# Sorted edge groups in pairs, selected by quarters, with 16-bit destinations and one 16-bit bias pass

## The chip, the core and the metric

The program runs on one core of one Trainium2 chip. A core has a matrix engine (PE, with its weight loads shown as PEld), a vector engine (DVE), a scalar engine (ACT), a third compute engine (POOL, which here issues the indirect gathers) and a sync engine (SP, which here issues DMAs). Each engine works through its own list of instructions in order and waits on semaphores. The metric is the device time of one execution in microseconds (us); lower is better.

## The reference

A graph layer with 6,250 nodes, 100,000 edges sorted by destination, 128 features and 4 edge attributes, in 32-bit floats:

```python
msg_in = concatenate([x[src], x[dst], edge_attr], axis=1)
h = silu(msg_in @ mW1 + mb1)
aggregated = segment_sum(h @ mW2 + mb2, dst, num_segments=6250)
u = silu(concatenate([x, aggregated], axis=1) @ uW1 + ub1)
out = _layernorm(x + layer_norm(x + u @ uW2 + ub2, ln_g, ln_b))
```

Here `layer_norm` normalises over the features, scales by `ln_g` and adds `ln_b`, and `_layernorm` is the same without scale and shift.

## The kernel before

The first product is split: table A is `x @ mW1[:128]` and table B is `x @ mW1[128:256] + mb1`, each with one row for each node. Edges are cut into 98 groups of 1,024 (`GE`), each of 8 tiles of 128. Because destinations are sorted, the destinations of a group lie in a window of 80 rows (`W`) of table B, and its sums go into a window of 80 columns of an accumulator.

There are two ways to get a group's rows of table A.

- A *listed* group (78 of them) gathers: eight indirect DMAs on POOL (`fetch`, line 243) bring 128 rows each. PE adds the destination part and the attributes (`before_rows`, `pre<-mv,st`: a one-hot matrix `st` of the destinations, made by DVE at line 603 from the row `near`, times 80 rows of table B). DVE adds the two (line 655), ACT applies silu (line 657), and `sums` multiplies the result by the one-hot matrix `oh` into `pt`, which `add` puts into the accumulator.
- A *sorted* group (20 of them, every fourth from 15 on: `Q0, QD, QN = 15, 4, 20`) has its edges sorted by source at the start of the run, so that the edges of each tile of 128 source nodes lie in a narrow window of positions (`window`, line 119). PE then selects rows without a gather: for every tile `b` of 128 nodes that can occur, it multiplies the tile of table A by a one-hot matrix `O` of the keys, over the columns of the window, into the bank `po`. Table A is held as three 16-bit parts, so each window takes three products (`select`, line 1080). The position range is cut into two halves of 512, and a window that crosses the cut is worked in two pieces.

The one-hot matrices `O` of a sorted group are made by `picks` (two of four by DVE at line 1052, two by ACT at lines 1056 and 1057). Its attributes enter through `attribute_part` (a 512-wide 32-bit product of `at_s` and `Oc`, and a DVE step at line 1068 that writes into `st_s`), the destination part through `begin_half`; silu is at line 1099, and `turned_hidden` transposes the result back (line 1107) and copies it (line 1108).

The order is written out by hand. The loop at line 1212 has one stage for each listed group. In a stage the loads for later groups are issued on SP (`sorted_ahead`, then `load`), then come the matrices of the group two ahead, `before_rows` and `hidden` of the next one, the pieces of a sorted group (`sorted_before`), the sums of this group, `sorted_behind`, and steps for a batch of 512 nodes (`node_stage`). A sorted group `k` is spread over the six stages before its own place: loads six stages ahead, matrices five, first attribute part four, both quarters of the first half three, one quarter of the second half two, the last quarter one stage ahead, sums at its place. So its pattern has a period of three stages, in which four groups are done. Gathers are paced: `paced` (line 1277) ties every second one to a product on PE some 3.5 groups earlier.

Once for each batch of nodes (line 735) `node_y` opens a bank with the bias row `ub2`: a 32-bit product of a row of ones with a row that holds `ub2` four times.

Of the kernel before, what the change touches and what calls it, by code (L numbers as in the profile page):

```python
# [10 lines left out]
F32 = mybir.dt.float32  # L11
# [10 lines left out]
P = 128  # L22
# [5 lines left out]
def kernel(  # L28
# [57 lines left out]
    Q0, QD, QN = 15, 4, 20  # L86
    by_sort = {Q0 + QD * q: q for q in range(QN)}
# [6 lines left out]
    SORTED = Q0 - 7  # L94
    S0 = 96
    HB = GE // 2
    SLACK = 400.0
# [13 lines left out]
    def made_for(g):  # L111
        stage = stage_of(g) - 5 if g in by_sort else turn_of(g) - LEAD
        return max(k for k in range(NB) if k < 2 or x_stage(k) + 2 < stage)
# [5 lines left out]
    def window(b, half):  # L119
# [4 lines left out]
        lo = max(floor(edge(b * P, -1)), half * HB)  # L124
        hi = min(ceil(edge(min(b * P + P - 1, N - 1), 1)) + 1, half * HB + HB)
        return lo, hi
# [106 lines left out]
    sd = dram.tile([4, QN * GE], F16, name="sd")  # L233
    ea_d = dram.tile([ED, NG * GE], F32, name="ea_d")
# [97 lines left out]
    def lists_1():  # L332
# [4 lines left out]
        nc.vector.tensor_scalar(rel_n, dst_l, base_c, None, op0=OP.subtract)  # L337
        parts.update(base_c=base_c, rel_n=rel_n, rel_t=rel_t)
# [101 lines left out]
    def destinations(g):  # L440
        near[g] = work.tile([P, GE], I32, name="near")[:W]
        n = min(GE, E - g * GE)
        if n < GE:
            nc.vector.memset(near[g][:, n:], N)
# [85 lines left out]
    ub2_row = consts.tile([1, BN, H], F32, name="ub2_row")  # L530
    late = {}

    def weights():
# [4 lines left out]
        nc.sync.dma_start(mb2_col, mb2.rearrange("(f o) -> f o", o=1))  # L538
        nc.sync.dma_start(
            ub2_row, ub2.rearrange("(o i f) -> o i f", o=1, i=1).to_broadcast([1, BN, H])  # L540
# [5 lines left out]
    def merged():  # L546
# [9 lines left out]
        nc.scalar.copy(bc_row, pb[0:1, :H])  # L556

# [6 lines left out]
    for k in range(NST + 1):  # L564
        ohbuf.append(kept.tile([P, G, WS if k < NST else W], F32, name=f"oh{k}"))
# [33 lines left out]
    def matrices(g):  # L599
        if g >= NG:  # L600
# [5 lines left out]
            base_p[:W, g : g + 1],  # L606
# [128 lines left out]
    def node_y(k):  # L735
# [3 lines left out]
        matmul(py[:, :n], ones[0:1, :], ub2_row[:, :n], start=True, stop=False)  # L739
# [81 lines left out]
    def turned_lists():  # L821
        pt = selected()
        for f, of in enumerate((src_i, rel)):
            picked = first.tile([P, QN, G], F32, name="picked")
            nc.vector.tensor_copy(picked, of[:, Q0 : Q0 + QN * QD : QD, :])
# [135 lines left out]
    def prepare():  # L961
        pool = edges.enter_context(tc.tile_pool(name="sel", bufs=1, side="right"))
        t = {
            "O": lambda: pool.tile([P, G // 2, HB], BF16, name="O", bufs=3),
            "sc": lambda: pool.tile([P, 2, GE], F16, name="sc", bufs=2),
            "ar": lambda: pool.tile([P, GE], F16, name="ar"),
            "h": lambda: pool.tile([P, G, H], F32, name="h_s"),
            "hT": lambda: pool.tile([P, HB], F32, name="hT", bufs=2),
        }
        t["Oc"] = pool.tile([P, GE], F32, name="Oc")  # L970
        t["st"] = pool.tile([P, GE], F32, name="st_s")
        t["mv"] = [pool.tile([P, H], F32, name=f"mv_s{k}") for k in range(2)]
        t["at"] = pool.tile([P, P], F32, name="at_s")
        nc.vector.memset(t["st"][S0 - 32 : S0], 0.0)
        for m in t["mv"]:
            nc.vector.memset(m[S0 - 32 : S0], 0.0)
        nc.vector.memset(t["at"][:, :S0], 0.0)
# [34 lines left out]
    def load_sorted(g):  # L1012
        t, q = sel[0], by_sort[g]
        cols = slice(q * GE, (q + 1) * GE)
        now["sc", g] = t["sc"]()
        nc.sync.dma_start(
            now["sc", g], sd[0:2, cols].rearrange("(o f) e -> o f e", o=1).to_broadcast([P, 2, GE])
        )
        now["ar"] = t["ar"]()
        nc.sync.dma_start(now["ar"][:W], sd[3:4, cols].to_broadcast([W, GE]))  # L1020
        nc.sync.dma_start(now["ar"][S0:], sd[2:3, cols].to_broadcast([P - S0, GE]))
        nc.sync.dma_start(
            t["at"][:, S0:],
            edge_attr[g * GE : (g + 1) * GE].rearrange("(c a) d -> c (a d)", a=G),
        )

    def load_rows(g):
        t, q = sel[0], by_sort[g]
        need_bases(g)
        nc.sync.dma_start(t["mv"][q % 2][:W], tab_b[bass.ds(bases[g], W), :])  # L1030

    def sorted_matrices(g):
        t = sel[0]
        nc.vector.tensor_scalar(
            t["st"][:W],
            now["ar"][:W],
            p_col[:W],
            0.0,
            op0=OP.is_equal,
            op1=OP.add,  # L1040
            accum_out=deg_col(g),
        )
        nc.vector.tensor_scalar(t["Oc"], now["sc", g][:, 1], p_col, None, op0=OP.is_equal)

    def picks(g, c):
        half, r0 = c // 2, c % 2 * (G // 2)
        O = sel[0]["O"]()
        key = now["sc", g][:, 0, half * HB : (half + 1) * HB]
        for j in range(G // 2):
            r = r0 + j  # L1050
            if j < 2:
                nc.vector.tensor_scalar(  # L1052
                    O[:, j], key, p_rows[:, r : r + 1], None, op0=OP.is_equal
                )
            else:
                nc.scalar.activation(O[:, j], key, AF.Square, bias=p_less[:, r : r + 1])  # L1056
        nc.scalar.activation(O[:, 2:], O[:, 2:], AF.Relu, bias=ones[:, 0:1], scale=-1.0)  # L1057
        now[c] = O
# [494 lines left out]
```

## Time and profile before

| what | value |
|---|---|
| median of 3 runs | 1014.65 us (1009.31 to 1018.19) |
| time of the profiled execution | 1012.41 us |
| its span, first to last instruction | 1010.6 us |
| mean granted PE clock | 0.896 |
| PE busy / weight loads busy | 812.3 us / 694.0 us, 7154 instructions each |
| DVE / ACT / POOL busy | 581.8 / 456.9 / 612.4 us |
| DMA moved | 108.69 MB |

The page's busy times of PE are those of instructions whose ends are modelled, and neighbours overlap; the distance between the starts of two products says more. In a group's row the mean duration of one follows the busy time, then the idle time of the engine just before such instructions and what ended most of it; "issue" there means that the engine waited for nothing that the profile shows.

### The profile page before, as it was taken

How to read it: one execution, taken by the hardware profiler on the slowest of the kernel's cores; microseconds unless marked ns; L12 is line 12 of the kernel's file. 1: busy time of each engine (PE TensorE's matmuls, PEld its weight loads, DVE VectorE, ACT ScalarE, POOL GpSimd, SP SyncE). 2: the span in 40 equal slices, each digit the busy share in tenths (PEclk: the TensorE clock that was granted, in tenths of full speed). 3: DMA queues.
4: the chain of work that ended last, by engine and by line, in shares of the span. 5: the costliest groups of instructions: out<-in, count | busy, mean ns of one | idle time of the engine just before them, and what ended most of it. 6: DMA issues, size and time to landing. Idle time of an engine off the chain costs nothing.

```text
span 1010.6 us, 19484 instructions
## 1 busy us (share of the span) xinstructions
PE 812.3 (80%) x7154; PEld 694.0 (69%) x7154; DVE 581.8 (58%) x1464; ACT 456.9 (45%) x685; POOL 612.4 (61%) x633
## 2 busy tenths in 40 slices
PE   5557546888988878978978978878989888978884
PEld 4547536676777677767767768667777687767673
DVE  3465687964564664744755654754764664654464
ACT  1122113563545545545554554564554564454343
POOL 6656655866666665666665666666666666565650
PEclk8769777888999999988998999999989989899977
DMA  9554323542443443533533533542533633423321
GB/s 219 136 146 113 100 72 78 139 128 76 120 116 95 121 117 94 133 99 89 137 100 82 148 97 89 139 114 78 162 94 86 149 93 93 122 60 86 91 61 30
DMA packets 87568, 108.69 MB, mean 108 GB/s; under 512 B 22044, under 2 KB 63504, under 8 KB 87466
## 3 DMA queue, kind: packets, MB, share of 16 engines
q1 hardware_dynamic: 54194, 60.01, 21.6%
q0 software_dynamic: 19904, 40.80, 16.8%
q10 hardware_dynamic: 13368, 6.56, 2.4%
q8 instruction: 58, 0.95, 0.4%
q14 instruction: 44, 0.36, 0.1%
HBM read 95.88 MB, written 11.43 MB: 106 GB/s over the span
## 4 chain that ended last, share of the span: by engine, by line
PE 64%; issue 13%; DVE 11%; ACT 4%; another core or an unknown queue 3%; DMA 2%; SPq 1%; POOL 1%; DVEq 1%; ACTq 0%; POOLq 0%
PE po L152 22%; PE pt L152 16%; PE pre L152 12%; PE pn L152 10%; PE pn L155 2%; DVE ga L655 2%; PE pre L155 1%; DVE y L760 1%; ACT O L1056 1%; DVE bn L716 1%; DVE z L785 1%; ACT O L1057 1%; DVE var L717 1%; DMA near<-in_dst_dram 1%
## 5 line engine op out<-in xcount | busy, mean ns | idle before, releaser
L243 POOL DMA_INDIRECT ga<-tab_a,src_i x582 | 572.4, 983 | 349.9 <-issue 155.9
L152 PE MATMUL po<-O,A_low 128*128 128x144 bf16 (+25 forms) x1120 | 209.7, 227 | 11.2 <-issue 11.2
L152 PE MATMUL po<-O,A 128*128 128x147 bf16 (+37 forms) x1720 | 177.5, 230 | 39.1 <-issue 22.8
L152 PE MATMUL pre<-mv,st 128*128 128x128 f32 x1244 | 179.0, 293 | 25.8 <-DVE st L603 8.2
L152 PEld LDWEIGHTS pre<-mv,st 128*128 128x128 f32 x1244 | 164.2, 206 | 39.5 <-issue 17.9
L152 PEld LDWEIGHTS pt<-oh,h 128*128 128x128 f32 x1244 | 164.7, 208 | 34.4 <-issue 32.5
L152 PE MATMUL pt<-oh,h 128*128 128x104 f32 x1244 | 173.0, 293 | 18.5 <-issue 14.2
L152 PEld LDWEIGHTS <-A 128*128 128x128 bf16 x1720 | 144.2, 106 | 57.4 <-issue 56.1
L703 DVE TENSOR_TENSOR acc<-acc,pt 128x80 f32 x98 | 23.0, 234 | 275.2 <-PE pre L152 120.4
L657 ACT ACTIVATE h<-ga 128x512 f32<-128x512 f32 x146 | 88.8, 627 | 190.4 <-DVE ga L655 108.9
L152 PEld LDWEIGHTS <-A_low 128*128 128x128 bf16 x1120 | 115.4, 104 | 16.7 <-issue 16.6
L655 DVE TENSOR_TENSOR ga<-ga,pre 128x512 f32<-128x512 f32 x146 | 94.3, 676 | 32.0 <-PE pt L152 9.0
L603 DVE TENSOR_SCALAR_CACHE_REDUCE st<-near,base_p 80x1024 f32<-80x1024 int32 x78 | 98.4, 1261 | 14.5 <-issue 9.2
L1056 ACT ACTIVATE O<-sc,p_less 128x512 bf16<-128x512 f16 x160 | 105.5, 706 | 0.0
L1057 ACT ACTIVATE O<-O,ones 128x1024 bf16<-128x1024 bf16 x80 | 91.8, 1148 | 2.6
L1099 ACT ACTIVATE hT<-po 128x512 f32<-128x512 f32 x40 | 23.5, 587 | 108.3 <-PE po L152 39.9
L613 DVE TENSOR_TENSOR oh<-w_row,rel 128x640 f32<-128x640 f32 x78 | 63.6, 816 | 0.6
L152 PE MATMUL po<-O,A_high 128*128 128x51 bf16 (+12 forms) x520 | 49.4, 217 | 16.6 <-issue 16.4
L152 PEld LDWEIGHTS <-A_high 128*128 128x128 bf16 x520 | 38.0, 99 | 28.9 <-issue 28.9
L243 POOL DMA_INDIRECT ga<-in_x_dram,src_i x40 | 38.3, 957 | 23.0 <-issue 10.4
L152 PE MATMUL pn<-Oc,at_s 128*128 128x512 f32 x80 | 47.9, 683 | 4.1 <-issue 4.1
L1052 DVE TENSOR_SCALAR O<-sc,p_rows 128x512 bf16<-128x512 f16 x160 | 49.8, 362 | 0.0
(221 smaller groups left out, 921.0 us busy)
## 6 DMA issues: line engine op xcount, KB each, us to landing
near<-in_dst_dram SPq DMA_DIRECT2D x77, 320.0 KB
sc<-sd SPq DMA_DIRECT2D x20, 512.0 KB
ga<-tab_a,src_i POOLq DMA_INDIRECT x582
ar<-sd SPq DMA_DIRECT2D x20, 160.0 KB
mv<-tab_b SPq DMA_DIRECT2D x78, 40.0 KB
tab_a<-A SPq DMA_DIRECT2D x11, 256.0 KB
tab_b<-o SPq DMA_DIRECT2D x11, 256.0 KB
out_dram<-o ACTq DMA_DIRECT2D x11, 256.0 KB
```

The source lines that it names most:

```text
L152: counted(nc.tensor.matmul(to, *operands, **flags), to, share)
L155: counted(nc.tensor.transpose(to, *operands), to)
L243: ins = nc.gpsimd.indirect_dma_start(out=rows[g][:, i, :], out_offset=None, in_=x if g < RAW else tab_a[:, :], in_offset=bass.IndirectOffs ...
L603: nc.vector.tensor_scalar(stbuf[turn_of(g) % NST][:W], near.pop(g), base_p[:W, g : g + 1], 0.0, op0=OP.is_equal, op1=OP.add, accum_out=deg ...
L613: nc.vector.tensor_tensor(oh[g][:, :n, :W], w_row[:, None, :].to_broadcast([P, n, W]), rel[:, g, :n, None].to_broadcast([P, n, W]), op=OP. ...
L655: nc.vector.tensor_add(s[:, i], s[:, i], of)
L657: nc.scalar.activation(h[:, i], of, AF.Silu)
L703: nc.vector.tensor_add(to, to, pt[:, :W])
L1052: nc.vector.tensor_scalar(O[:, j], key, p_rows[:, r : r + 1], None, op0=OP.is_equal)
L1056: nc.scalar.activation(O[:, j], key, AF.Square, bias=p_less[:, r : r + 1])
L1057: nc.scalar.activation(O[:, 2:], O[:, 2:], AF.Relu, bias=ones[:, 0:1], scale=-1.0)
L1099: nc.scalar.activation(now["hT", half], now.pop("po"), AF.Silu)
```

## The change

Sorted groups are now neighbours, two at a time: 17 and 18, 25 and 26, up to 89 and 90. They are still 20. A pair is worked together, by four quarters of 256 positions of each of the two groups. One product covers the same window in both groups: its columns are two runs, one in each. A pair is spread over stages 8 to 0 before its place, and the pattern has a period of six stages, in which eight groups are done. Quarter `u` is loaded at `at_stage[u] + 3`, its matrices are made at `+ 2`, its one-hot matrices and attribute part at `+ 1`, and it is selected 5, 4, 2 and 1 stages ahead.

Three smaller edits go with it. The destinations relative to a group's first one are written once to DRAM as 16-bit floats, and `near` is loaded from there (it was loaded as 32-bit integers from `dst`), so line 603 compares with `p_col` and not with `base_p`. The bias row `ub2` is held as three 16-bit parts on three partitions, and the opening product of `node_y` is one 16-bit pass. Buffers: `O` has four (three before), `st_s` and `at_s` two each, `ar` two, `h_s` is for two groups, `oh` has one more.

```diff
-    Q0, QD, QN = 15, 4, 20
-    by_sort = {Q0 + QD * q: q for q in range(QN)}
+    Q0, QD, QN = 17, 8, 20
+    firsts = [Q0 + QD * q for q in range(QN // 2)]
+    by_sort = {k + u: 2 * q + u for q, k in enumerate(firsts) for u in range(2)}
...
+    QB = GE // GR
+    at_stage = (5, 4, 2, 1)
...
+        rel_h = first.tile([P, GE], F16, name="rel_h")
+        nc.scalar.copy(rel_h[:NG], rel_n)
+        nc.sync.dma_start(near_d, rel_h[:NG])
...
-        nc.sync.dma_start(
-            near[g][:, :n],
-            dst[g * GE : g * GE + n].rearrange("(o e) -> o e", o=1).to_broadcast([W, n]),
-        )
+        near[g] = work.tile([P, GE], F16, name="near")[:W]
+        nc.sync.dma_start(near[g], near_d[g : g + 1].to_broadcast([W, GE]))
...
+        rows = late.pop("rows")
+        part = first.tile([96, H], BF16, name="ub2_part")
+        nc.scalar.copy(ub2_rows[0:1], rows[0:1])
+        nc.scalar.copy(part, rows)
+        nc.vector.tensor_sub(rows, rows, part)
+        nc.scalar.copy(ub2_rows[32:33], rows[32:33])
+        nc.scalar.copy(part, rows)
+        nc.vector.tensor_sub(ub2_rows[64:65], rows[64:65], part[64:65])
...
-        matmul(py[:, :n], ones[0:1, :], ub2_row[:, :n], start=True, stop=False)
+        matmul(
+            py[:, :n], ones_16, ub2_rows[:, None, :].to_broadcast([P, n, H]),
+            start=True, stop=False, share=1 / 4,
+        )
...
+    def load_part(k, u):
...
+        for f in range(2):
+            nc.sync.dma_start(
+                sc[:, f], of[f].rearrange("(o g) c -> o g c", o=1).to_broadcast([P, 2, QB])
+            )
...
+    def sorted_matrices(k, u):
         t = sel[0]
+        for v in range(2):
+            nc.vector.tensor_scalar(
+                t["st"][u % 2][:W, v * QB : (v + 1) * QB],
+                now["ar", u][:W, v],
+                p_col[:W],
+                0.0,
+                op0=OP.is_equal,
+                op1=OP.add,
+                accum_out=t["deg"][:, v, u : u + 1],
+            )
...
+        if u == GR - 1:
+            for v in range(2):
+                nc.vector.tensor_reduce(deg_col(k + v), t["deg"][:, v], AX.X, OP.add)
...
+    def select(u):
         t = sel[0]
+        po = now["po"] = selected()
+        for v in range(2):
+            cols = slice(v * QB, (v + 1) * QB)
+            matmul(po[:, cols], t["mv"][v], t["st"][u % 2][:, cols], start=v == 0, stop=False)
+        to = po.rearrange("p (g c) -> p g c", g=2)
         todo = []
...
+        for part_r in range(2):
+            O = now.pop(("O", u, part_r)).rearrange("p r (g c) -> p r g c", g=2)
+            r0 = part_r * (G // 2)
+            for b in range(NT):
+                if r0 <= b % G < r0 + G // 2:
+                    lo, hi = window(b, u)
+                    if lo < hi:
+                        cols = slice(lo - u * QB, hi - u * QB)
+                        for a in parts_of(b):
+                            todo.append((to[:, :, cols], a, O[:, b % G - r0, :, cols]))
+        for n, (to, a, of) in enumerate(todo):
+            matmul(to, a, of, start=False, stop=n == len(todo) - 1, share=1 / 3)
...
     def sorted_before(j):
...
+        for u, d in enumerate(at_stage):
+            for _ in pair_at(j, d + 1):
+                picks(u)
+        for k in pair_at(j, 0):
+            for v in range(2):
+                add(k + v, sums(k + v))
+        for u, d in enumerate(at_stage):
+            for k in pair_at(j, d - 1):
+                if u < GR - 1:
+                    turned_hidden(k, u)
+        for u, d in enumerate(at_stage):
+            for _ in pair_at(j, d):
+                select(u)
+                sorted_hidden(u)
+        for u, d in enumerate(at_stage):
+            for _ in pair_at(j, d + 1):
+                attribute_part(u)
+        for k in pair_at(j, 1):
+            for v in range(2):
+                sorted_oh(k + v)
```

More of the change, by code (lines that the diff above doesn't have):

```diff
@@ L1045, in picks @@
[L1045 to L1058, printed above, removed]
+            ar[S0:], of[2].rearrange("(o g) c -> o g c", o=1).to_broadcast([P - S0, 2, QB])
+        )
@@ new lines, in picks @@
+    def picks(u):
+        key = now.pop(("sc", u))[:, 0].rearrange("p g c -> p (g c)")
+        for part_r in range(2):
+            O = sel[0]["O"]()
+            for j in range(G // 2):
+                r = part_r * (G // 2) + j
+                if j < 2:
+                    nc.vector.tensor_scalar(
+                        O[:, j], key, p_rows[:, r : r + 1], None, op0=OP.is_equal
+                    )
+                else:
+                    nc.scalar.activation(O[:, j], key, AF.Square, bias=p_less[:, r : r + 1])
+            nc.scalar.activation(O[:, 2:], O[:, 2:], AF.Relu, bias=ones[:, 0:1], scale=-1.0)
+            now["O", u, part_r] = O
```

209 lines of the change are left out of this document (86 added, 123 removed).

## The prediction, made before the changed kernel was run

> **What bounds the kernel now.** I read the page first, then the engines' busy time between the 13th and the 73rd listed group, then single selections in the timeline, then the waits of PE and POOL.
>
> ```profile
> PE 812.3 (80%) x7154; PEld 694.0 (69%) x7154; DVE 581.8 (58%) x1464; ACT 456.9 (45%) x685; POOL 612.4 (61%) x633
> ...
> PE 64%; issue 13%; DVE 11%; ACT 4%; another core or an unknown queue 3%; DMA 2%; SPq 1%; POOL 1%; DVEq 1%; ACTq 0%; POOLq 0%
> ...
> L243 POOL DMA_INDIRECT ga<-tab_a,src_i x582 | 572.4, 983 | 349.9 <-issue 155.9
> L152 PE MATMUL po<-O,A_low 128*128 128x144 bf16 (+25 forms) x1120 | 209.7, 227 | 11.2 <-issue 11.2
> L152 PE MATMUL po<-O,A 128*128 128x147 bf16 (+37 forms) x1720 | 177.5, 230 | 39.1 <-issue 22.8
> ...
> L152 PE MATMUL po<-O,A_high 128*128 128x51 bf16 (+12 forms) x520 | 49.4, 217 | 16.6 <-issue 16.4
> ```
>
> The chain that ended last is PE for 64%, and 13% of the span (131 us) is "issue", time in which the waiting engine waited for nothing visible. The selections are 1120 + 1720 + 520 = 3360 products, 168 for each sorted group.
>
> ```profile
> core 0: us, PE busy (x) PEld busy (x) DVE busy (x) ACT busy (x) POOL busy (x), PEclk, DMA share, GB/s
> ...
> 213.00:960.30 747.30, 646.96 (x6124) 548.66 (x6122) 418.25 (x1002) 377.52 (x565) 465.98 (x479) 0.94 0.41 106
> ```
>
> From the sums of the 13th listed group at 213.0 to those of the 73rd at 960.3 there are 60 stages, ten times eight groups: 74.7 us for eight groups, my unit below. Only PE looks full, but what is it full of? The starts of products in two selections tell:
>
> ```profile
> 416.38 0.20 PE L152 MATMUL po<-O,A 128*128 128x19 bf16 x2
> ...
> 416.46 0.20 PE L152 MATMUL po<-O,A 128*128 128x40 bf16 x2
> ...
> 417.03 0.30 PE L152 MATMUL po<-O,A 128*128 128x156 bf16 x2
> ...
> 417.23 0.30 PE L152 MATMUL po<-O,A 128*128 128x155 bf16 x2
> ```
> ```profile
> 429.27 0.21 PE L152 MATMUL po<-O,A_high 128*128 128x51 bf16 x2
> ...
> 431.25 0.23 PE L152 MATMUL po<-O,A 128*128 128x78 bf16 x2
> ...
> 431.87 0.23 PE L152 MATMUL po<-O,A 128*128 128x57 bf16 x2 [0.35 <-issue]
> ...
> 432.62 0.21 PE L152 MATMUL po<-O,A 128*128 128x36 bf16 x2 [0.49 <-issue]
> ...
> 433.33 0.18 PE L152 MATMUL po<-O,A_low 128*128 128x36 bf16 x1 [0.50 <-issue]
> ...
> 434.78 0.22 PE L152 MATMUL po<-O,A_high 128*128 128x110 bf16 x1 [1.14 <-issue]
> ```
>
> Three products of 156 columns take 0.20 us, 67 ns each (0.43 ns a column); three of 19 columns take 0.08 us, 27 ns each. So PE pays by the column down to about 27 ns. The second selection runs like that from 429.27 for 13 windows (39 products, 78 instructions with their loads) and then stops: at 431.87, 432.62, 433.33 and 434.78 it sits idle, after only three to five products each time. No semaphore is named. I read this as instructions arriving late: a run of narrow products uses them up at about 78 in 2.6 us, 30 per us, and then gets some 8 to 10 per 0.7 us, 13 per us. Over the 747.3 us PE took 6124 products and as many loads, 16.4 per us: the whole stretch goes at close to the rate of the starved part.
>
> ```profile
> PE po L152 <- issue: 46.9, 81, 2.3
> PE po L152 <- ACT O L1057: 16.0, 8, 2.3
> PE pt L152 <- issue: 11.3, 20, 1.1
> PE pre L152 <- DVE st L603: 5.6, 5, 3.7
> PE pn L155 <- DVE st_s L1068: 5.2, 4, 2.4
> PE pre L152 <- issue: 4.7, 10, 0.9
> ```
>
> In the same stretch such gaps end 111 waits of PE, 62.9 us beyond the modelled ends. A product's row lasts about 0.2 us where the next could start after 0.05, so each gap hides some 0.15 us more: 62.9 + 111 x 0.15 = 80 us, 8 for eight groups. Semaphores account for 16.0 + 5.6 + 5.2 = 26.8 us, 2.7 for eight groups.
>
> **Eight groups on PE, from rows.**
>
> ```profile
> 478.62 0.91 PE pn L152 x8
> ...
> 488.90 2.99 PE pn L152 x6
> 491.88 1.78 PE pre L152 x16
> ...
> 495.97 0.94 PE pn L152 x2
> 496.91 1.76 PE pt L152 x16
> 498.67 3.02 PE pn L152 x12
> 501.69 0.44 PE pn L155 x4
> ```
>
> Six listed groups: 6 x (1.78 + 1.76) = 21.2. Two sorted ones: sums 80 and not 104 columns wide, 2 x 1.35 = 2.7; four 512-wide attribute products 4 x 0.94 = 3.8 and four destination products of that shape, 3.8; four transposes 1.8; selections: the window formula gives 19,587 columns a group, 2 x 19,587 x 0.43 ns = 16.8, with the 27 ns floor of narrow pieces 17.5. One batch of nodes: 2.99 + 0.91 + (3.02 - 0.94) + 0.44 (four transposes of x) + 0.2 (the transposed counts) = 6.6. Sum 57.4 of 74.7. The other 17.3: the granted clock of 0.94 means half speed in 12% of the time, 4.5 us; semaphores about 3; the gaps 8; 2 not assigned.
>
> **The change, part by part.**
>
> *Selection.* By the window formula the columns stay exactly the same (39,174 a pair). The pieces go from 56 a group (112 a pair) to 70 a pair, so products from 336 to 210 a pair and from 3360 to 2100 in all: 117 columns each before, 187 after, 0.08 us for two instructions, 25 per us. By columns alone that is worth only the floors of narrow pieces, 0.4 us a pair. By instructions, eight groups go from 622 products (counted in the code; 612 a unit recorded) to 622 - 126 + 16 (destination and attribute products are cut in two) - 1 = 511, 82%. A selection is now at most 57 products, 114 instructions in 4.8 us, where two quarters used to run together, 84 products. Take 13 to 16.4 per us as the supply; then 78 - 2.6 x 13 = 44 to 78 - 2.6 x 16.4 = 35 were in store, and 4.8 us have 44 + 4.8 x 13 = 106 to 35 + 4.8 x 16.4 = 114 of the 114: just enough, or one gap. I take 2 us of gaps for eight groups in place of 8, and 1 of the 2 unassigned. Bounds: all 8 stay, or none. A product over two runs of columns does not occur before; its bounds are no cost and one floor more, 210 x 27 ns = 5.7 us a pair. I take no cost, since pieces of 19 to 156 columns show no price beyond columns and floor.
>
> The Trainium skill, TensorE: Matmul & The Clock Gate, section Back-to-back issue gap, gives columns/2.4 + 2.5 ns between matmuls at full clock; the dense rows agree (156 columns: 67.5 ns). By that rule alone the pairing is worth 126 x 2.5 ns, an estimate of 0.3 us a pair: it speaks against this change.
>
> *Row ub2.* Two 512-wide passes of 0.94 / 2 become one 16-bit pass, 512 x 0.43 ns = 0.22: 0.7 us a batch, one batch a unit.
>
> *DVE.*
>
> ```profile
> L1034 DVE TENSOR_SCALAR_CACHE_REDUCE st_s<-ar,p_rows x20: 1264/1268/1271, 191.1 to 905.4; 80x1024 f32<-80x1024 f16 x20
> L1043 DVE TENSOR_SCALAR Oc<-sc,p_rows x20: 740/745/892, 192.3 to 906.6; 128x1024 f32<-128x1024 f16 x20
> ```
>
> A pair had 2 x (1.27 + 0.08 + 0.75) = 4.2 us of these; it gets eight 256-wide ones (0.32 by size, at most 0.6; I take 0.45, plus 0.08), four 512-wide ones (0.37 to 0.75; 0.5) and two small reductions (0.2): 6.6 us, 2.4 more, at the end of four of six stages. DVE goes from 41.8 to 44.2 us a unit, two thirds of 66: hidden behind PE, except where PE waits for the next `st`; 0.5 us. The first row reads 16 bits and takes what line 603 takes for 32, so the new `near` saves nothing on DVE.
>
> *ACT.* `picks` and silu keep their number and size. They come as two `O` in each of four stages: 2 x (2 x 0.71 + 1.15) = 5.1 us beside silu and copies of 2.4, 7.5 of an 11 us stage, selected one stage later as before. The late steps of a node batch (tables, output) fall four stages before a pair's place, where no `picks` stands. I leave its wait, 1.6 us a unit, as it is.
>
> *SP and DMA.* A pair's DMAs on SP go from 10 to 20, about 0.35 us each to issue: 3.5 us a unit on an engine that mostly waits. They stand ahead of `load` in each stage and wait for `ar` and `sc` of two quarters before, free by the end of the stage before; `near`, `mv` and `st` behind them are needed a stage later. Cover: that stage, 11 us; without it the landing, 2 to 3 us, would show in DVE's `st` and so in `pre`. `near` moves half the bytes. I take 0 (bounds -1 and +3 us a unit).
>
> *Start.* A copy to 16 bits (about 1 us on ACT), one 200 KB store that the first `near` waits for, and seven small steps for `ub2` (about 2.5 us): once, beside the tables; 0, at most +6. The ends of the run keep their stages.
>
> **Sum.** 57.4 - 0.4 - 0.7 = 56.3; clock 4; semaphores 3 + 0.5; gaps 2; unassigned 1: 66.8, and I take 66 because gaps also bring on the low clock. 74.7 - 66 = 8.7, times ten: 87 us. The profiled execution took 1012.41 us (0.2% under the median of 1014.65): 1012.4 - 87 = 925 us.
>
> **Gathers beside it.**
>
> ```profile
> 402.52 0.94 POOL L243 DMA_INDIRECT ga<-tab_a,src_i  x1 [0.30 <-issue]
> ...
> POOL ga L243 <- remote: 42.4, 31, 1.7
> ```
>
> A gather costs at least 0.94 + 0.30 us; by the mean 0.98 + 0.30, 48 for eight groups are 61.4 us, 65.7 with the unknown waits of 42.4 / 10. That is late next: under 66 the gathers set the pace, so little more than forecast is to be had.
>
> **Rivals.**
>
> *The gaps stay.* If they do not come from the number of instructions (another engine's traffic, a place in the program), pairing saves 0.4 + 0.7 us a unit: 1012 - 11 = 1001, from 990 to 1010. For it: 84-product runs sometimes pass without a gap. Against it: gaps sit after some 80 instructions of a dense run, with no semaphore. The Trainium skill, Runtime: NRT & Kernel Launch, section Instruction fetch mechanics, holds that fetching is hidden, since dispatch (some 20 cycles an instruction) is slower than the refill; by that rule this rival is right, and the rows at 431.87 to 433.33 do not look like it.
>
> *Gathers bound.* If they stay at 65.7 and meet PE's waits badly, some 69 a unit: 1012 - 57 = 955.
>
> *Slower: `O` comes late.* Two `O` take 5.1 us of ACT in a stage where one or two stood. If each of a pair's four selections waits more than 8.7 / 4 = 2.2 us for ACT, the gain is gone; at 3.5 us each it is 14 - 8.7 = 5.3 a unit, 1012 + 53 = 1065. For it: the wait is there now (16.0 us, up to 2.3). Against it: ACT is busy for 377.52 of 747.30 us.
>
> **Chances.** Forecast 0.66 (own range 895 to 960), gathers bound 0.09, gaps stay 0.15, slower 0.10. About 1% is what a measurement of this kernel tells from no change. Faster by over 1% (under 1004.5): 0.66 + 0.09 + a third of 0.15 = 0.80; within 1% 0.09; slower 0.11. The low end, 890, is gathers without a wait (61.4 a unit: 1012 - 133 = 879) nearly reached; the high end, 1000, takes in most of "the gaps stay".
>
> **What would show it.** Right: 2100 selection products, their idle time by "issue" down from 50.4 us (11.2 + 22.8 + 16.4) to under 20; granted clock above 0.90; POOL's share of the span at 66% or more. Wrong: "issue" unchanged beside 2100 products; `po` waiting for ACT over 40 us; a product over two runs taking visibly more than its columns.

## The result: slower, and where the time went

| | before | changed |
|---|---|---|
| median of 4 runs each | 1016.42 us (1009.31 to 1018.29) | 1077.88 us (1074.53 to 1082.12) |
| profiled execution, its span | 1012.41, 1010.6 us | 1078.77, 1077.0 us |
| mean granted PE clock | 0.896 | 0.859 |

The ratio is 1.062 (95% interval 1.058 to 1.067): some 62 us slower, where 87 us faster was forecast. The page of the changed kernel (busy times, the chain of waits) and its groups by line show it; line numbers moved, so the matmul helper is now line 155, transposes are line 158, the add into the accumulator is line 716.

```profile
PE 817.7 (76%) x6041; PEld 720.4 (67%) x6041; DVE 594.5 (55%) x1629; ACT 458.4 (43%) x690; POOL 611.0 (57%) x633
...
PE 54%; DVE 19%; issue 12%; another core or an unknown queue 6%; POOL 3%; ACT 2%; DMA 2%; DVEq 1%; ACTq 0%; POOLq 0%; SPq 0%
```
```profile
L155 PE MATMUL po<-O,A_low 128*128 128x314 bf16 (+54 forms) x700 | 156.0, 246 | 7.1 <-issue 6.9
L155 PE MATMUL po<-O,A 128*128 128x216 bf16 (+37 forms) x1060 | 143.8, 246 | 12.9 <-issue 12.8
...
L155 PE MATMUL po<-O,A_high 128*128 128x102 bf16 (+16 forms) x340 | 46.3, 246 | 4.3 <-issue 4.3
```

The selections did what the change says: 700 + 1060 + 340 = 2,100 products, with 24.0 us of idle time by "issue" where the three rows of before sum to 50.4. But the chain of waits runs 19% through DVE (11% before) and 54% through PE (64%). The list of PE's waits (us in total, times, longest) names what is new:

```profile
PE pn L158 <- DVE st_s L1109: 45.5, 10, 6.0
PE pt L155 <- DVE acc L716: 30.1, 10, 5.1
PE po L155 <- issue: 24.0, 43, 1.1
...
PE pn L155 <- DVE Oc L1078: 22.7, 8, 3.3
```

Three waits of PE for DVE, 45.5 + 30.1 + 22.7 = 98.3 us, each about once for each of the ten pairs. In the same list of before, `st_s` stands with 5.2 us, the wait for `acc` with 2.4 and Oc not at all. And over ten units, from the sums of the 13th listed group to those of the 73rd, the unit grew from 74.7 to 80.9 us, with the granted clock down from 0.94 to 0.89:

```profile
core 0: us, PE busy (x) PEld busy (x) DVE busy (x) ACT busy (x) POOL busy (x), PEclk, DMA share, GB/s
212.40:1021.70 809.30, 653.57 (x5035) 574.81 (x5033) 431.04 (x1154) 377.84 (x565) 461.51 (x480) 0.89 0.34 87
```

The first theory was therefore: the selections became shorter, and the order of the pair's stages made round trips between PE and DVE (PE waits until DVE has read its bank, and only then goes on) that nothing covers. Stages are named here by their distance d to the pair's place. The pair selects at d = 5, 4, 2 and 1, and not at 3 and 0. At the end of d = 4 and in d = 3 DVE has the second normalisation of a node batch, in d = 0 PE has two sums of the pair through the one buffer of `pt`. The experiments take these apart.

### The profile page after: what moved, and what is told of

The parts are those of the page before. It is cut to its first block, busy times and chain, and to the rows that moved or that the text cites. A ratio compares the mean times of both kernels' runs of the same rounds, so it can differ in the third digit from the quotient of the medians.

```text
span 1077.0 us, 17602 instructions
## 1 busy us (share of the span) xinstructions
PE 817.7 (76%) x6041; PEld 720.4 (67%) x6041; DVE 594.5 (55%) x1629; ACT 458.4 (43%) x690; POOL 611.0 (57%) x633
## 4 chain that ended last, share of the span: by engine, by line
PE 54%; DVE 19%; issue 12%; another core or an unknown queue 6%; POOL 3%; ACT 2%; DMA 2%; DVEq 1%; ACTq 0%; POOLq 0%; SPq 0%
PE po L155 16%; PE pt L155 14%; PE pre L155 12%; PE pn L155 8%; POOL ga L247 3%; PE pn L158 3%; DVE ga L668 2%; DVE O L1092 2%; DMA ga<-tab_a,src_i 2%; DVE st L616 2%; DVE oh L626 1%; DVE bn L729 1%; DVE z L801 1%; DVE var L730 1%
## 5 line engine op out<-in xcount | busy, mean ns | idle before, releaser
L155 PE MATMUL po<-O,A_low 128*128 128x314 bf16 (+54 forms) x700 | 156.0, 246 | 7.1 <-issue 6.9
L155 PE MATMUL po<-O,A 128*128 128x216 bf16 (+37 forms) x1060 | 143.8, 246 | 12.9 <-issue 12.8
L155 PEld LDWEIGHTS <-A 128*128 128x128 bf16 x1060 | 88.6, 97 | 32.1 <-issue 18.1
L616 DVE TENSOR_SCALAR_CACHE_REDUCE st<-near,p_rows 80x1024 f32<-80x1024 f16 x78 | 98.4, 1262 | 11.0 <-issue 9.8
L1109 DVE SCALAR_TENSOR_TENSOR st_s<-ar,part,pn 32x512 f32<-32x512 f16 x40 | 30.2, 756 | 117.1 <-PE pn L155 83.7
L155 PEld LDWEIGHTS <-A_low 128*128 128x128 bf16 x700 | 67.6, 98 | 18.5 <-issue 11.8
L155 PE MATMUL pt<-oh,h_s 128*128 128x80 f32 x320 | 51.3, 323 | 35.2 <-DVE acc L716 29.8
L155 PEld LDWEIGHTS pt<-oh,h_s 128*128 128x128 f32 x320 | 47.9, 235 | 37.8 <-DVE acc L716 31.1
L155 PE MATMUL pn<-Oc,at_s 128*128 128x256 f32 x160 | 52.3, 457 | 25.6 <-DVE Oc L1078 22.7
L155 PEld LDWEIGHTS pn<-Oc,at_s 128*128 128x128 f32 x160 | 31.8, 221 | 30.6 <-remote 23.3
```

Of the source, the lines that this page charges most:

```text
L155: counted(nc.tensor.matmul(to, *operands, **flags), to, share)
L616: nc.vector.tensor_scalar(stbuf[turn_of(g) % NST][:W], near.pop(g), p_col[:W], 0.0, op0=OP.is_equal, op1=OP.add, accum_out=deg_col(g),)
L1109: nc.vector.scalar_tensor_tensor(t["st"][u % 2][S0:], now.pop(("ar", u))[S0:].rearrange("p g c -> p (g c)"), part[S0:], px[S0:], op0=OP.is ...
```

## Experiments on the parts

All ratios are to the kernel before on the same chip; differences of ratios are turned into us with 1016. The first four ask which part costs.

**e1: the same pairs, each product cut in two again**

```diff
-                            todo.append((to[:, :, cols], a, O[:, b % G - r0, :, cols]))
+                            for v in range(2):
+                                todo.append((to[:, v, cols], a, O[:, b % G - r0, v, cols], share))
```

> The changed kernel with each selection product over two groups cut again into one product for each group: 4,200 products in place of 2,100, the same columns in the same order, everything else as it is. Theory (the loss comes from round trips between PE and DVE that the grouping into pairs creates, and the number of products matters only inside the selections): the idle time of the selections by 'issue' comes back from 24 to 50 us or more and the time rises by 20 to 70 us, because PE is the bound in the stages that select, while the waits of PE for DVE (x transposes 45.5 us, second sums 30.1, Oc 22.7) stay or shrink by the slack that PE loses. Rival (the number of instructions is worth nothing and fewer products saved nothing): within 10 us of the changed kernel. Rival (the two-run product itself is slow and is the loss): the split kernel is faster than the changed one by 30 us or more.

Ratio 1.102 (1.096 to 1.107), so 40 us above the changed kernel; the selections' idle time by "issue" went to 72.0 us, and of the three waits for DVE that for Oc is down to 0.4 us; that the longer selections cover it is the likely reason and was not tried alone. The pairing of products saves something here, and all else that came with the pairs costs at most about 100 us (1.102 against 1; e1 has 840 products more than the kernel before, and their price is in it).

**e2: the small edits alone, on the kernel before**

```diff
-        near[g] = work.tile([P, GE], I32, name="near")[:W]
+        near[g] = work.tile([P, GE], F16, name="near")[:W]
+        nc.sync.dma_start(near[g], near_d[g : g + 1].to_broadcast([W, GE]))
...
-        matmul(py[:, :n], ones[0:1, :], ub2_row[:, :n], start=True, stop=False)
+        matmul(
+            py[:, :n], ones_16, ub2_rows[:, None, :].to_broadcast([P, n, H]),
+            start=True, stop=False, share=1 / 4,
+        )
```

> The kernel before with the two small edits alone: destinations in 16 bits from DRAM, and the row ub2 by one 16-bit pass; no pairs. Theory (the loss is all in the pairing): 0 to 12 us faster than before, about 1008. Rival (the 16-bit destinations bring a longer start or later one-hot matrices, and with them a part of the loss): slower than before by 10 us or more.

Ratio 0.999 (0.996 to 1.003). Together they cost nothing and bring nothing that can be seen; the loss is in the pairs.

**e3: both sums of a pair, then both adds**

```diff
-            for v in range(2):
-                add(k + v, sums(k + v))
+            both = ps1.tile([P, 4 * P], F32, name="pt")
+            half = [both[:, 2 * P * v : 2 * P * v + 2 * P] for v in range(2)]
+            for v in range(2):
+                sums(k + v, half[v])
+            for v in range(2):
+                add(k + v, half[v])
```

> The changed kernel with the sums of both groups of a pair in two halves of one bank, both sums first and then both adds, in place of sum, add, sum, add through one buffer. Theory (each DVE round trip is a wait that nothing covers): the wait of the second sums for the first add (30.1 us, ten times 3) is gone and the time falls by 15 to 30 us, to about 1053. Rival (PE only runs up against something else, such as the gathers or DVE's total): the 30 us show up in other waits and the time stays within 8 us.

Ratio 1.035 (1.030 to 1.040): 28 us less than the changed kernel, as the theory said. The wait itself fell from 30.1 to 13.8 us and did not vanish: what is left stands before the next group's sums, which take the same bank after both adds.

**e4: the second normalisation one stage later**

```diff
-            if j == u + 2:
+            if j == u + 3:
                 r = inverse(0, 2 * BN, k)
                 node_z(k, r)
```

> The changed kernel with the second normalisation of a node batch (DVE's inverse and node_z, and ACT's output steps) one stage later, so that it ends in front of a stage that selects, not in front of the stage without a selection. Theory: the x transposes' wait for DVE (45.5 us in ten) falls under 15 and the time falls by 20 to 40 us. Rival (the wait comes from the selection's own DVE work, picks and attribute part, and not from the node batch): the wait stays over 30 us and the time within 8 us. Third possibility: the wait only moves to the stage after, same time and another line in the list of waits.

Ratio 1.037 (1.032 to 1.041), 26 us less. The waits show that the theory holds for the larger part only:

```profile
PE pn L155 <- remote: 25.0, 8, 3.3
PE pn L158 <- issue: 24.8, 11, 5.4
...
PE pn L158 <- DVE st_s L1109: 10.7, 6, 3.7
```

The transposes' wait for DVE fell from 45.5 to 10.7 us. The row with "remote" is the wait for Oc under another name: its eight products begin 0.15 us after the end of Oc's step, as the eight of the changed kernel do. The 24.8 us in front of transposes are new, and the list names no cause; in the trace eight of these eleven waits, 23.0 us, are transposes of a selection's result that begin 0.05 us after ACT has ended its silu (line 1137). So a part of the wait went over to ACT.

**e5 and e6: a third bank for `pn`, and its control**

For a third bank the row of column numbers leaves the bank that it has to itself; e5 does that alone.

```diff
-    w_row = ps1.tile([P, W], F32, name="w_row")
+    w_row = kept.tile([P, W], F32, name="w_row")
...
-        return ps1.tile([P, BN, P], F32, name="pn", bufs=2)
+        return ps1.tile([P, BN, P], F32, name="pn", bufs=3)
```

> Control for the next run: the changed kernel with the row of column numbers (`w_row`, 80 numbers that DVE compares with) in SBUF in place of a PSUM bank of its own; nothing else. Theory and rivals agree: within 8 us of the changed kernel (ratio to before 1.055 to 1.070), the waits of PE as they are.

> As the control, with the bank that came free given to `pn`, which so has three buffers in place of two. Theory (the x transposes stand still because the bank they want is held until DVE has done the step of attribute_part): their wait of 45.5 us falls under 10 and the time falls by 20 to 45 us against the control. Rival (PE would only wait a little later for the same DVE work): the wait is gone from this row and comes back on other rows, with the time within 8 us of the control.

Control 1.072 (1.068 to 1.076), with the third bank 1.036 (1.028 to 1.043): 37 us between them. The control is itself some 10 us above the changed kernel, a little more than expected, so e6 lies 27 us under the changed kernel. No wait of the x transposes for `st_s` is left in the list of e6 (42.6 us in e5): what they waited for was the bank.

**e7: all pairs one group later**

```diff
-    Q0, QD, QN = 17, 8, 20
+    Q0, QD, QN = 18, 8, 20
```

> The changed kernel with the first pair at group 18 in place of 17, all pairs one group later, so that the node batches (every eighth group) fall one stage earlier within a pair's six stages; nothing else. The node batch's DVE work then runs into a stage that selects. Theory: the x transposes' wait for DVE falls under 15 us and the time falls by 15 to 45 us. Rival (any order of these stages has the same waits, the pairs alone are the cause): within 8 us of the changed kernel.

Ratio 1.016 (1.012 to 1.020): one number, 47 us less, a little over the range. No row for x transposes that wait for `st_s` is left in the list, and Oc is down to 1.7 us. A part has moved: 20.7 us (listed as 11.8 for `O` and 8.9 for `st_s`) stand before products of the node batch that need the same bank. The pair's sums still wait:

```profile
PE pt L155 <- DVE acc L716: 32.4, 11, 5.1
...
PE pn L155 <- DVE Oc L1078: 1.7, 2, 0.9
```

**e8: three changes of order together**

e3 and e4, and `attribute_part` moved from `sorted_before` to the head of `sorted_behind`.

> The changed kernel with three changes of order together: both sums of a pair into two halves of one bank before both adds (as in e3), the second normalisation one stage later (as in e4), and attribute_part behind the sums and the add of its stage and not ahead of them, so that its Oc has time. Theory (three waits of some 10 us a pair in all, each created by the order of the pair's stages): 28 + 26 + 15 to 20 us less than the changed kernel, 1005 to 1025 on the scale where the changed one takes 1078 and the one before 1016. Rival (the gains are not additive, since each only uncovers the next bound): no better than 1050.

Ratio 1.015 (1.012 to 1.018), 49 us less: no more than e3 and e4 bring together (54), and 1031 on the scale of the expectation, 6 us above its upper end. Oc is gone from the list, but the x transposes wait for `st_s` again, so the third change seems only to have handed the wait on (e11 tries it alone):

```profile
PE pn L158 <- DVE st_s L1109: 27.6, 10, 5.0
```

**e9 to e11: the two mends that hold, and two more on top**

e9 is e7 with e3. e10 adds the third bank of e6 to it, e11 the later `attribute_part` of e8.

> The changed kernel with the pairs one group later (as in e7) and both sums of a pair ahead of both adds (as in e3). Theory (separate waits, separate gains): the 32.4 us of 'pt waits for acc' in e7 fall under 17 and the time falls by 15 to 28 us against e7, which puts it at 0.99 to 1.003 of the kernel before. Rival (the gains share one bound, such as the gathers or the low clock): within 8 us of e7, 1.016.

> As e9, with the row of column numbers in SBUF and three buffers of pn. Theory: with the pairs one group later the x transposes hardly wait for DVE any more, so the third bank buys little: 0 to 15 us against e9, and the move of the row costs some 5 to 10 us (e5 against the changed kernel), so within 10 us of e9. Rival (pn is short in any order): 15 us or more under e9.

> As e9, with attribute_part behind the sums and the add of its stage. Theory: e7 has only 1.7 us of waits for Oc, but 11.8 + 8.9 us in which pn waits for DVE's picks and step of attribute_part; putting it later gives DVE time for both: 5 to 15 us under e9, so level with the kernel before or a little under it. Rival (as e8 showed: the wait is handed to the x transposes): 0 to 10 us above e9.

e9: 0.994 (0.991 to 0.997), 70 us under the changed kernel, where e3 and e7 alone brought 28 and 47: separate waits, nearly additive. It is a little faster than the kernel before. Waits are left in it: 30.0 us before products of the node batch for the bank (listed as 18.0 for `O` and 12.0 for `st_s`), 10.6 for `acc`. e10: 0.994 (0.990 to 0.997), so the third bank, with the move of the row that cost some 10 us in e5, gives nothing on top. The wait for the bank is gone from its list, and the wait of `pt` for `acc` went from 10.6 to 27.6 us. e11: 1.001 (0.998 to 1.005), the rival's side.

**e12: the third bank on the kernel before**

> Control on the kernel before: the row of column numbers in SBUF and three buffers of pn, nothing else. Theory (before, PE waits only 5.2 us for DVE at pn, so a third bank has nothing to give): from 3 us faster to 12 us slower, the latter by the move of the row as in e5. Rival (a third bank helps any version, and e6 tells nothing of the pairs): 15 us or more faster.

Ratio 0.998 (0.994 to 1.002). Bank and move together were worth 27 us to the changed kernel and are worth nothing to the one before, where even without the cost of the move (some 10 us in e5) the bank would bring far less than 37: the want of it came with the pairs.

## Experiments on the gaps

With the largest waits mended the pairs are level with the kernel before, not 87 us ahead. So what are fewer products worth? e13 is e9 with the products of e1; e14 and e15 are controls of place.

> The kernel of e9 (pairs one group later, both sums ahead of both adds) with each selection product cut into one for each group, 4,200 in place of 2,100, as in e1. If the number of products limits PE in the selections as the prediction said (8 us of gaps for eight groups that go to 2), the time rises by 50 to 90 us against e9, to 1.04 to 1.08 of the kernel before. If it is worth what e1 against the changed kernel suggests (40 us for 2,100 products, 11 of them the floor of narrow pieces), 30 to 45 us: 1.02 to 1.04. If the count hardly matters, under 15 us.

e14 is the kernel before with one edit:

```diff
-    Q0, QD, QN = 15, 4, 20
+    Q0, QD, QN = 16, 4, 20
```

> Control: the kernel before with its sorted groups one group later (first at 16 in place of 15, every fourth as it was), nothing else. Theory (the place of the node batch matters in the pairs because two of their six stages have no selection; before, with one sorted group in three stages, no such stage meets it): within 10 us of the kernel before. Rival (the shift helps any order, so e7 and e9 say nothing of the pairs): 20 us or more faster.

e15 is e9 with the second normalisation at `j == u + 1`.

> The kernel of e9 with the second normalisation of a node batch one stage earlier, right behind the first. Theory (DVE and ACT work of the batch now ends in the stage that has PE's sums of the pair and no selection, with nothing to cover it): 5 to 30 us slower than e9. Rival (any other place is as good, or better because it leaves the stages with picks): 0 to 10 us faster than e9.

These three ran on one chip, and e16 to e18 on another, on which the kernel before takes 850 us and not 1016. Ratios: e13 1.017 (1.011 to 1.022), e14 1.011 (1.004 to 1.018), e15 1.056 (1.050 to 1.061). So the shift by one group is no gain in itself there (e14 is slower if anything), and the place of the node batch is worth some 44 us to the mended kernel too (e15; more than the 5 to 30 expected). e13 lies below both ranges that give the number of products a price. To have all of it beside each other, the changed kernel, the mended one and the mended one with split products were put on one chip:

> The changed kernel itself, once more, beside e17 and e18 on one chip. Theory (its loss is PE's waits for DVE, which do not depend on the chip; the gaps in the selections do): where the selections show no gaps (kernel before near 850 us), the changed kernel loses as much or more, 50 to 110 us, ratio 1.06 to 1.13, since it has no gaps to save; where they show gaps (kernel before near 1015 us), 1.05 to 1.07 as before. Rival (the pauses of PE are what makes the pairs slow): on a chip without gaps within 1% of the kernel before.

> The kernel of e9 again (pairs one group later, both sums ahead of both adds), beside e16 and e18. Theory: 0.99 to 1.00 of the kernel before on a chip with gaps, and 1.00 to 1.02 on one without, where fewer products save nothing but floors. Rival (fewer products are worth the same on every chip): 0.985 to 0.997 on both.

> The kernel of e13 again (e9 with 4,200 selection products in place of 2,100). If the number of products costs only where PE has gaps: 5 to 15 us above e17 on a chip without gaps (11 of them by the floor of narrow pieces), 30 to 60 us above e17 on one with gaps. If it costs the same everywhere: 30 us or more on both.

| kernel, products | median | ratio to before (850.52 us) |
|---|---|---|
| e16, changed, 2,100 | 943.10 us | 1.109 (1.103 to 1.116) |
| e17, mended, 2,100 | 852.81 us | 1.002 (0.999 to 1.005) |
| e18, mended and split, 4,200 | 863.42 us | 1.016 (1.010 to 1.022) |

**The gaps belong to the chip.** The groups of e18, with twice the products, and of e14, the kernel before but for the shift:

```profile
L155 PE MATMUL po<-O,A_low 128*128 128x157 bf16 (+54 forms) x1400 | 165.0, 206 | 0.0
L155 PE MATMUL po<-O,A 128*128 128x108 bf16 (+37 forms) x2120 | 151.8, 207 | 0.0
...
L155 PE MATMUL po<-O,A_high 128*128 128x94 bf16 (+16 forms) x680 | 45.4, 204 | 0.0
```
```profile
L152 PE MATMUL po<-O,A_low 128*128 128x144 bf16 (+25 forms) x1120 | 187.2, 217 | 0.0
L152 PE MATMUL po<-O,A 128*128 128x147 bf16 (+37 forms) x1720 | 147.3, 215 | 0.3 <-ACT O L1057 0.3
L152 PE MATMUL po<-O,A_high 128*128 128x51 bf16 (+12 forms) x520 | 48.9, 227 | 0.0
```

No idle time at all in 4,200 products, none by "issue" in 3,360, and none in the 2,100 of e16 and e17. e18 is 10.6 us above e17, and the floor of 27 ns for narrow pieces, by the window formula, gives an estimate of 1.15 us a pair or 11.5 us in all. Within the spread of the runs, some 5 us, nothing is left over for the number of instructions on this chip. On the others the gaps go with the number of products: 20.6 to 35.2 us by "issue" in the profiles with 2,100, 50.4 to 60.3 in the three with 3,360 (before, e2, e12), 72.0 with 4,200. The Trainium skill, Runtime: NRT & Kernel Launch, section Instruction fetch mechanics, which the prediction set aside, holds that fetching is hidden; the 0.0 here agree with it.

What are the gaps on the other chips, then? The same place in the timeline of the changed kernel, there and in e16: a listed group's sums, and the add that needs only the last of them. First the profile of the result:

```profile
548.83 2.02 PE L155 MATMUL pt<-oh,h 128*128 128x104 f32 x16 [0.49 <-PE po L155]
...
554.86 0.24 DVE L716 TENSOR_TENSOR acc<-acc,pt 128x80 f32 x1 [5.96 <-remote]
```

Then e16:

```profile
549.09 1.95 PE L155 MATMUL pt<-oh,h 128*128 128x104 f32 x16
...
551.08 0.24 DVE L716 TENSOR_TENSOR acc<-acc,pt 128x80 f32 x1 [3.61 <-PE pt L155]
```

In e16 the add begins 0.04 us after the recorded end of the sums (549.09 + 1.95), in the other profile 4.01 us after it (548.83 + 2.02), though DVE had been idle for 5.96 us; the view can name no releaser but "remote". This is no single case. Take every add into the accumulator before which DVE sat idle, and count from the recorded end of its sums: 24 of 63 in the kernel before and 22 of 64 in the changed one begin over 0.9 us late (up to 5.4 and 4.1 us of it idle); in e16, e17 and e18 none of 67, 56 and 57 begins over 0.11 us late. What waits for DVE is not late: the ten waits of the x transposes for `st_s` in the changed kernel end 0.06 us after that step, as in e16. A reading that fits is that on those chips PE stands still for some us now and then while its records run on, since their ends are computed and not seen; a gap by "issue" could then be the moment when no further instruction can be handed to a PE that has stopped. The Trainium skill, Perfetto Trace Analysis, section Tensor Engine Instruction (MATMUL, LD_WEIGHTS), says that the profiler estimates a matmul's end, and the 4.01 us fit that. That late adds and gaps come and go together is shown; that PE itself pauses, that the gaps are these pauses, and why on some chips only, was not tried.

The traces of those chips also lack records of signals (the semaphore events by which the views name who ended a wait): 647 for 743 matmuls that signal in the kernel before, 769 for 772 in e16. There a name in the list of waits can be missing or wrong, as in e4.

**The round trips belong to the kernel.** The changed kernel loses 92.6 us on this chip, more than on the chip of the result, and the mended one next to nothing. Two of its three waits are there at about the same size:

```profile
PE pn L158 <- DVE st_s L1109: 48.6, 9, 5.9
PE pt L155 <- DVE acc L716: 32.5, 11, 5.0
```

In the mended kernel (e17) the first is gone from the x transposes, with 16.2 us left before another product of the node batch, and the second is 1.8 us. The third, for Oc, is not in e16's list: in the profile of the result Oc came late behind late adds such as the one at 554.86, so those 22.7 us go with the chip as well as with the order. One period of six stages, d = 5 to d = 0, each row from the sums of one stage to those of the next (us, then busy time and instructions of each engine, clock, DMA). First e16:

```profile
core 0: us, PE busy (x) PEld busy (x) DVE busy (x) ACT busy (x) POOL busy (x), PEclk, DMA share, GB/s
525.91:538.13 12.22, 12.22 (x97) 9.73 (x95) 6.79 (x16) 6.52 (x10) 7.57 (x8) 0.99 0.37 99
538.13:549.09 10.96, 10.96 (x109) 9.99 (x107) 7.78 (x21) 3.25 (x5) 8.22 (x10) 1.00 0.59 153
549.09:553.99 4.90, 4.90 (x43) 4.80 (x42) 2.88 (x13) 2.27 (x4) 3.68 (x5) 1.00 0.18 44
553.99:573.34 19.35, 13.50 (x103) 12.15 (x102) 13.44 (x39) 16.28 (x24) 10.17 (x12) 0.82 0.31 83
573.34:582.89 9.55, 9.55 (x98) 9.19 (x97) 6.27 (x10) 1.70 (x3) 7.38 (x8) 1.00 0.54 119
582.89:597.03 14.14, 11.22 (x75) 10.71 (x74) 6.92 (x21) 8.79 (x14) 8.74 (x9) 0.79 0.40 101
```

Then e17:

```profile
core 0: us, PE busy (x) PEld busy (x) DVE busy (x) ACT busy (x) POOL busy (x), PEclk, DMA share, GB/s
484.72:494.92 10.20, 10.20 (x99) 9.73 (x98) 8.64 (x26) 2.13 (x4) 7.81 (x8) 1.00 0.54 137
494.92:508.95 14.03, 11.36 (x98) 9.87 (x97) 9.51 (x30) 11.25 (x17) 9.07 (x10) 0.88 0.43 114
508.95:514.27 5.32, 5.32 (x47) 5.22 (x46) 3.45 (x11) 2.34 (x5) 4.10 (x5) 1.00 0.32 82
514.27:527.04 12.77, 11.54 (x107) 10.27 (x106) 9.44 (x26) 11.30 (x17) 9.72 (x11) 1.00 0.47 118
527.04:535.67 8.63, 8.63 (x91) 8.27 (x89) 6.51 (x13) 5.05 (x9) 6.50 (x8) 1.00 0.73 178
535.67:547.21 11.54, 11.54 (x83) 9.34 (x80) 6.42 (x17) 5.95 (x10) 8.74 (x10) 1.00 0.21 56
```

DVE is busy for 44 us in both periods. In e16, 13.44 of them and 16.28 of ACT's 38.8 fall into one stage, the one after the stage that doesn't select; it takes 19.35 us where the mended kernel's takes 12.77, and the stage of the two sums 14.14 against 11.54. The six rows sum to 71.12 and 62.49 us, 8.6 more; over all ten units it is 712.0 and 623.8 us, 88.2 of the 90.3 between the medians. Of the 8.6, 4.9 are idle time of PE (8.77 and 3.90); in the rest of the time PE is busy with 525 matmuls in both, for 62.35 and 58.59 us. The rows with the long waits have the low clock, 0.82 and 0.79. Around the start of that stage, e16:

```profile
552.03 0.48 DVE L1078 TENSOR_SCALAR Oc<-sc,p_rows 128x512 f32<-128x512 f16 x1
552.43 1.13 DVE L776 SCALAR_TENSOR_TENSOR y<-y,var,g_b 128x128 f32<-128x128 f32 x4
...
553.99 1.93 PE L155 MATMUL pt<-oh,h 128*128 128x104 f32 x16
...
556.44 1.24 DVE L616 TENSOR_SCALAR_CACHE_REDUCE st<-near,p_rows 80x1024 f32<-80x1024 f16 x1
...
559.54 1.38 DVE L1092 TENSOR_SCALAR O<-sc,p_rows 128x512 bf16<-128x512 f16 x4
...
560.95 0.76 DVE L1109 SCALAR_TENSOR_TENSOR st_s<-ar,part,pn 32x512 f32<-32x512 f16 x1
...
561.76 1.11 PE L158 MATMUL pn<-ident,x 128*128 128x128 f32 x4 [5.85 <-DVE st_s L1109]
```

From 551.08 to 561.71 DVE works without a pause, 10.6 us: an add, the matrices of a quarter with Oc, the normalisation (552.43 to 556.44), the next group's matrices, the adds of `pre`, picks, and last the step that frees the bank. The sums at 553.99 are those of the stage that doesn't select (d = 3); with no selection in front of them PE is done at 555.92 and waits for 5.85 us.

## Why the prediction was wrong, step by step

- **Products and columns:** right, 2,100 products. By the window formula the floors of narrow pieces are worth 0.1 us a pair, not the 0.4 of the sum; cutting the products in two costs about what the floors give (10.6 us in e18). The Trainium skill, TensorE: Matmul & The Clock Gate, section Back-to-back issue gap, from which the prediction took columns/2.4 + 2.5 ns, gives it for a single matmul and says that it under-counts in a stream of loads and products; the rows here agree with the formula all the same (67 ns for 156 columns).
- **"I read this as instructions arriving late", gaps 8 to 2 a unit:** the direction came true, the size did not, and the cause stays open. Gaps by "issue" fell from 50.4 to 24.0 us (33.1 in e9), 2.6 a unit where 6 were taken, and on those chips they go with the number of products: 2,100 more cost 40 us there (e1), of which some 11.5 are floors. But on the other chips there is no gap at 2,100, 3,360 or 4,200. So the number of instructions alone makes no gap, and the supply of 13 to 16 instructions per us that the prediction took from the gaps is no property of the kernel. The rival "the gaps stay" had it right for the quick chips, where the number makes no gap, and not for the others. A sign stood in the profile of before, 24 of 63 adds that begin late. The views show it only faintly, by 3% of the chain under "another core or an unknown queue" on a program of one core (all of it in the first 145 us), and by this row of DVE's waits, of which one wait, 8.2 us, is an add that begins 0.04 us after its sums and so isn't late:

```profile
DVE acc L703 <- remote: 32.5, 7, 9.8
```

- **DVE, "hidden behind PE ... 0.5 us":** this is the step that turned the sign. The sizes were near (rows of the profile after: the 256-wide matrices 0.469 + 0.079 us, Oc 0.477; in all DVE is 12.7 us busier, 1.3 a pair, where 2.4 was taken). But "two thirds of 66" is a mean over six stages, and two of them have lost the selection that covered DVE. The prediction had looked at the place of the node batch, four stages before the pair's, for ACT alone. Measured in place of 0.5 us a unit: 45.5 + 22.7 = 68.2 us in ten, 6.8 a unit; on the quicker chip the 48.6 of `st_s` alone.
- **Two sums in a row** through a one-buffer bank were not in the sum at all: 30.1 us of waits, 3.0 a unit, and 28 us by e3. Both steps together: 70 us back by e9, 90 on the other chip.
- **Clock:** 4 us a unit taken. The trace grants 1.0 or 0.5; a mean of 0.89 is half speed in 22% of the time and costs at most 11% of 80.9, 8.9 us, since a part of it falls into waits. In e16 the low clock stands in the rows with the waits; that they bring it on was not tried alone.
- **ub2:** 0.7 us a unit taken, nothing seen (e2). With these terms, 6.3 for DVE, 3.0 for the sums, at most 4.9 for the clock and 0.7 here, the unit comes from the forecast 66 to about the measured 80.9.
- **The slower rival** had its sign and no more: the wait of `po` for `O` from ACT, 16.0 us before, is gone from the list. That its 1065 us lie near the measured 1078 is luck. **Gathers** were no bound: POOL is busy for 57% of the span, not the 66% foretold, with the same work (611.0 us, 612.4 before) in a longer time.

The best version, e9, is 0.6% faster than the kernel before on one chip and equal on another (e17). What pairing brings is within about 1% either way in the orders tried here; e9 still has some 40 us of waits for a bank and e17 some 18, and what an order without them would give was not tried.

## What to carry to other kernels

When work is regrouped, lay out each stage of the new period by itself, with the longest chain of every engine in it; an engine at two thirds of a mean is the bound in the stage from which the other's work was taken. Follow each single-buffer bank through the new order: two uses in a row are a round trip. And before idle time "by issue" is given a cause in the program, compare the starts of what waits for PE with PE's recorded ends, and look on a second chip.

## What was not expected of the hardware

The same kernel took 850 us on two chips and 1015 to 1023 on others, and the changed one 943 against 1078. The rows of DVE and POOL are nearly the same on both (in the changed kernel a gather 981 ns and 975 in e16, the step that makes `oh` 815 on both), and so are PE's (246 and 245 ns for the products of `A_low`); what differs is that work behind PE begins late, the gaps, and a little the granted clock (0.859 and 0.875). In us, the same change cost more on the quicker chip, 92.6 against 62. That fits the 26 us by which the gaps fell on the other, and was not tried alone.
